# Neighbourhood attention with keys on partitions, and a runtime branch between two forms of it

## The chip, the core and the metric

The kernel runs on one core of a Trainium2 chip, everything in float32. A core has TensorE (PE in the profile; PEld is its loading of the stationary operand, "weights"), VectorE (DVE), ScalarE (ACT), GpSimd (POOL) and SyncE (SP), which here only issues DMAs. SBUF and PSUM have 128 partitions. The metric is device time in microseconds (us), lower is better.

## What is computed

The input `x` is (2, 56, 56, 256). Layer 0 normalises it in 32 groups, applies neighbourhood attention (8 heads of 32 channels, a 7x7 window that is shifted inwards at the border, a learned bias per relative position) and adds the result to `x`. Layer 1, which the change doesn't touch, is a chunked linear attention and a mixture of 8 experts. The part that matters, cut:

```python
x = fold_in(key(seed), 1) normal, (2, 56, 56, 256)       # setup_inputs
ks = split(key(seed), 5)
wq = normal(ks[1], (256, 256)) * 0.02                    # wk, wv, rpb: ks[2], ks[3], ks[4]; biases zero
...
q = (gn(x) @ wq.T + bq) / sqrt(32);  k = gn(x) @ wk.T + bk;  v = gn(x) @ wv.T + bv
scores = einsum('bnijd,bnijkd->bnijk', q, k_window) + bias_window
ctx = einsum('bnijk,bnijkd->bnijd', softmax(scores), v_window)
x = x + ctx
```

`fold_in`, `split` and `key` are those of `jax.random`.

## The kernel before

Three stages follow each other.

Projections (lines 166 to 276 of the file). The group statistics are taken, then for each batch and each block of 448 pixels the projections q, k (channels on partitions, L231) and v (pixels on partitions, L262) are multiplied. q is scaled by VectorE (L242), k is copied out by ScalarE (L251), v by VectorE (L269), and all three are written to DRAM (`q_d`, `k_d`, `v_d`).

Neighbourhood attention (L348 to L550). The image is cut into tiles of 8x14 queries: 7 strips of rows, 4 tiles in a strip, 2 batches, so 56 tiles; each has a frame of up to 14x20 = 280 keys. The bias is spread once through DRAM (`rpb_d`, L366 and L371) and added to a mask for each kind of tile on GpSimd (`bc`, L414). A unit is one tile and one group of 4 heads, 112 units. For each of its heads, `scores` multiplies queries by keys (L455: 32 rows of the array, 112 stationary columns, up to 280 moving ones), adds the bias and takes the row minimum of the negated scores in one VectorE instruction (L464), and takes the exponential with the row's sum on ScalarE (L474). `transposes` turns the exponentials with the array in two or three pieces for each head (L491) and copies them out of PSUM (L497, L499). `values` multiplies them with v (L510), and at the second group divides by the sums (L519, L521), adds `x` (L525) and writes `x1_d` with 8 DMAs from ScalarE's queue (L529). The last loop is a software pipeline over units: scores of unit n, transposes of n-1, values of n-2.

Layer 1 (from L551) reads `x1_d` (L618) and runs 14 steps; its chunk attention and the experts of earlier steps (L1170 to L1214) are interleaved by generators.

The loop that sets the order of the attention stage:

```python
for unit in chain(units(), (None, None)):
    if unit is not None:
        unit[0](unit[3])
    under_way.append(unit)
    if len(under_way) > 1 and under_way[-2] is not None:
        under_way[-2][1](under_way[-2][3])
    if len(under_way) > 2:
        done = under_way.pop(0)
        done[2](done[3])
```

Within an engine instructions run in the order in which the program lists them; across engines semaphores hold back whoever needs data or a buffer.

Of the kernel before, what the change touches and what calls it, by code (L numbers as in the profile page):

```python
# [32 lines left out]
QR, QC = 8, 14  # L33
TT = QR * QC
FR, FC = QR + WIN - 1, QC + WIN - 1
FK = FR * FC
NSR, NSC = IMG // QR, IMG // QC
# [35 lines left out]
def frame(start, size):  # L73

    lo, hi = max(start - WIN // 2, 0), min(start + size + WIN // 2, IMG)
    return lo, hi, lo - (start - WIN // 2)
# [6 lines left out]
def constants():  # L83
# [36 lines left out]
    mask = np.zeros((3, 3, TT, FK), np.float32)  # L120
    starts = (0, 1, -1)
    for er in range(3):
        r0 = QR * (starts[er] % NSR)
        rlo, rhi, _ = frame(r0, QR)
        for ec in range(3):
            c0 = QC * (starts[ec] % NSC)
            clo, chi, _ = frame(c0, QC)
            m = np.full((QR, QC, rhi - rlo, chi - clo), MASKED, np.float32)
            for a in range(QR):
                i = window_start(r0 + a) - rlo  # L130
                for b in range(QC):
                    j = window_start(c0 + b) - clo
                    m[a, b, i : i + WIN, j : j + WIN] = 0
            m = m.reshape(TT, -1)
            mask[er, ec, :, : m.shape[1]] = m
    c["nmask"] = mask
    return c


@with_exitstack  # L140
def hybrid_kernel(ctx: ExitStack, tc: tile.TileContext, t: dict, out: bass.AP):
# [5 lines left out]
    k_d = dram.tile([NB, C, L], F32, name="k_d")  # L147
    v_d = dram.tile([NB, IMG, IMG, C], F32, name="v_d")
    x1_d = dram.tile([NB, IMG, IMG, C], F32, name="x1_d")
    rpb_d = dram.tile([QC, NH, FR + QR - 1, FC], F32, name="rpb_d")  # L150
# [13 lines left out]

    with (
# [15 lines left out]
        bv = load(gp, "bv", [TT, C], t["L0_conv_bv"].unsqueeze(0).to_broadcast([TT, C]))  # L181

# [31 lines left out]
        for b in range(NB):  # L214
            for i in range(nst):
# [11 lines left out]
                for w, bias, dst, what in ((wq, bq, q_d, "q"), (wk, bk, k_d, "k")):  # L227
                    for g in range(NG):
# [9 lines left out]
                        o = ev.tile([P, BLK], F32, tag=f"ev{what}", name=f"ev{what}")  # L238
                        if what == "q":


                            nc.vector.tensor_scalar(  # L242
                                o.rearrange("p (q r c) -> p r q c", q=NSC, r=QR),
                                ps.rearrange("p (r q c) -> p r q c", q=NSC, r=QR),
                                bias[:, g : g + 1],
                                -1.0 / math.sqrt(HD),
                                ALU.add,
                                ALU.mult,
                            )
                        else:  # L250
                            nc.scalar.activation(  # L251
                                o, ps, AF.Identity, bias=bias[:, g : g + 1]
                            )
                        nc.sync.dma_start(
                            out=dst[b, g * P : (g + 1) * P, cols], in_=o
                        )
                o = ev.tile([TT, BLK // TT, C], F32, tag="evv", name="evv")
                for j in range(BLK // TT):
# [10 lines left out]
                    nc.vector.tensor_add(o[:, j, :], ps, bv)  # L269
# [4 lines left out]
                    in_=o,  # L274
                )

# [71 lines left out]
    with (  # L348
        tc.tile_pool(name="na1", bufs=1) as p1,
        tc.tile_pool(name="na", bufs=2) as p2,  # L350
        tc.tile_pool(name="na3", bufs=3) as p3,
        tc.tile_pool(name="na_sc", bufs=3, space=PSUM) as ps_s,
        tc.tile_pool(name="na_pt", bufs=3, space=PSUM) as ps_t,
        tc.tile_pool(name="na_po", bufs=2, space=PSUM) as ps_o,
    ):


        NR = 2 * WIN - 1
        pr, pc = QR - 1 - WIN // 2, QC - 1 - WIN // 2
        rp = p1.tile([NH, NR, NR], F32, name="rp")  # L360
        nc.sync.dma_start(out=rp, in_=t["L0_conv_rpb"])
        pad = p1.tile([NH, FR + QR - 1, FC + QC - 1], F32, name="pad")
        nc.gpsimd.memset(pad, 0.0)
        nc.vector.tensor_scalar_mul(pad[:, pr : pr + NR, pc : pc + NR], rp, -1.0)
        for b in range(QC):
            nc.sync.dma_start(  # L366
                out=rpb_d[b], in_=pad[:, :, QC - 1 - b : QC - 1 - b + FC]
            )
        bias = p1.tile([TT, NH, FR, FC], F32, name="bias")
        for a in range(QR):  # L370
            nc.sync.dma_start(  # L371
                out=bias[a * QC : (a + 1) * QC],
                in_=rpb_d[:, :, QR - 1 - a : QR - 1 - a + FR, :],
            )

        def units():

            for s in range(NSR):
                r0 = s * QR
                rlo, rhi, fr = frame(r0, QR)  # L380
                nr = rhi - rlo
                kw = p2.tile([P, NB, NG, FR * IMG], F32, tag="kw", name="kw")
                qw = p2.tile([P, NB, NG, QR * IMG], F32, tag="qw", name="qw")
                for b in range(NB):
                    nc.sync.dma_start(
                        out=kw[:, b, :, : nr * IMG],
                        in_=k_d[b, :, rlo * IMG : rhi * IMG].rearrange(
                            "(g p) l -> p g l", p=P
                        ),
                    )  # L390
                    nc.sync.dma_start(
                        out=qw[:, b],
                        in_=q_d[b, :, r0 * IMG : (r0 + QR) * IMG].rearrange(
                            "(g p) l -> p g l", p=P
                        ),
                    )
                last = bc = None
                for c in range(NSC):
                    clo, chi, fc = frame(c * QC, QC)
                    ncol = chi - clo  # L400
                    if edge(c, NSC) != last:
                        last = edge(c, NSC)
                        bc = tile_bias(edge(s, NSR), last, fr, nr, fc, ncol)
                    for b in range(NB):
                        yield from tile_units(
                            b, r0, c, rlo, nr, clo, ncol, kw[:, b], qw[:, b], bc
                        )

        def tile_bias(er, ec, fr, nr, fc, ncol):
            nk = nr * ncol  # L410
            msk = p2.tile([TT, FK], F32, tag="msk", name="msk")
            nc.sync.dma_start(out=msk, in_=t["nmask"][er, ec])
            bc = p2.tile([TT, NH, FK], F32, tag="bc", name="bc")
            nc.gpsimd.tensor_tensor(  # L414
                bc[:, :, :nk].rearrange("p h (r c) -> p h r c", c=ncol),
                bias[:, :, fr : fr + nr, fc : fc + ncol],
                msk[:, :nk]
                .rearrange("p (r c) -> p r c", c=ncol)
                .unsqueeze(1)
                .to_broadcast([TT, NH, nr, ncol]),  # L420
                ALU.add,
            )
            return bc

        def tile_units(b, r0, c, rlo, nr, clo, ncol, kw, qw, bc):
            c0, chi, nk = c * QC, clo + ncol, nr * ncol

            nj = -(-nr // (P // ncol))
            rows = [nr // nj + (j < nr % nj) for j in range(nj)]
            at = [sum(rows[:j]) for j in range(nj)]  # L430
            vw = p3.tile([P, 3, C], F32, tag="vw", name="vw")
            for j in range(nj):
                for r in range(rows[j]):
                    nc.sync.dma_start(
                        out=vw[r * ncol : (r + 1) * ncol, j, :],
                        in_=v_d[b, rlo + at[j] + r, clo:chi, :],
                    )
            xq = p3.tile([TT, C], F32, tag="xq", name="xq")
            for a in range(QR):
                nc.sync.dma_start(  # L440
                    out=xq[a * QC : (a + 1) * QC, :],
                    in_=t["x"][b, r0 + a, c0 : c0 + QC, :],
                )
            low = p3.tile([TT, NH], F32, tag="low", name="low")
            den = p3.tile([TT, NH], F32, tag="den", name="den")
            kept = {}

            def scores(g):
                sc = p2.tile([TT, 4, FK], F32, tag="sc", name="sc")
                ex = p3.tile([TT, 4, FK], F32, tag="ex", name="ex")  # L450
                for h in range(4):
                    hh = g * 4 + h
                    hp = slice(h * HD, (h + 1) * HD)
                    ps = ps_s.tile([TT, FK], F32, tag="ps", name="ps")
                    nc.tensor.matmul(  # L455
# [46 lines left out]
            def values(g):  # L502
# [14 lines left out]
                if g < NG - 1:  # L517
                    return
# [835 lines left out]
```

## Time and profile before

| | us |
|---|---|
| three runs | 3101.17, 3108.82 (median), 3118.96 |
| the profiled execution | 3124.91 |
| its span in the profile | 3122.9 |

| engine | busy in the span, us |
|---|---|
| PE (PEld) | 2450.1 (1729.7) |
| DVE | 1318.1 |
| ACT | 1033.5 |
| POOL | 646.4 |

The page's slices of the span show where the stages lie (each digit is one fortieth of the span, in tenths; PEclk is the clock granted to TensorE, 5 is half):

```
PE   6959978878797877767787887887887888885376
PEclk9955555555555555877888888888888898786688
DMA  5441111111112111000022222222222222123344
```

A float32 matrix product shows as two records of PE, a transpose as one. "Granted clock" is a share of the full clock. A table by stretches of the span gives, for each engine, busy microseconds and, in brackets, the number of instructions.

### The profile page before, as it was taken

Reading aid. Unit: us, or ns where it says so; the run is one execution under the profiler, and the core shown is the slowest. Engines: PE = TensorE matmul, PEld = TensorE weight load, DVE = VectorE, ACT = ScalarE, POOL = GpSimd, SP = SyncE. Lnnn points to the kernel's source line nnn. Section 1 sums busy time; section 2 is a strip of 40 time slices with the busy share of each in tenths; the row PEclk is TensorE's granted clock in tenths of the full one; section 3 lists DMA queues with packets and bytes.
Section 4 is the critical chain, followed back from the end, with each engine's and each line's share of the span. In section 5 each row is a group of like instructions: output and inputs, shape, how many; then the busy total and the mean of one; then the engine's idle time right before and its main releaser. Section 6 shows DMA issues by size and latency. Waiting matters only on the chain. (4 is left out here: it accounts for less than half of the span.)

```text
span 3122.9 us, 37893 instructions
## 1 busy us (share of the span) xinstructions
PE 2450.1 (78%) x13028; PEld 1729.7 (55%) x13028; DVE 1318.1 (42%) x4238; ACT 1033.5 (33%) x2268; POOL 646.4 (21%) x593
## 2 busy tenths in 40 slices
PE   6959978878797877767787887887887888885376
PEld 3647766767575766334454544555555555553254
DVE  5323323222222222566656556556655655651000
ACT  1123323232222222434344444444443544421011
POOL 0010011010101011121132232232233223222222
PEclk9955555555555555877888888888888898786688
DMA  5441111111112111000022222222222222123344
GB/s 206 150 112 30 30 59 30 52 37 40 46 28 61 27 58 37 1 25 17 9 81 64 49 80 64 53 78 64 62 68 66 63 65 82 42 68 105 95 111 104
DMA packets 136063, 196.50 MB, mean 63 GB/s; under 512 B 30368, under 2 KB 120432, under 8 KB 128192
## 3 DMA queue, kind: packets, MB, share of 16 engines
q1 hardware_dynamic: 100672, 153.58, 15.7%
q0 software_dynamic: 22368, 30.85, 5.8%
q10 hardware_dynamic: 12832, 9.66, 1.0%
q8 instruction: 104, 1.70, 0.2%
q14 instruction: 87, 0.71, 0.1%
HBM read 130.85 MB, written 63.14 MB: 62 GB/s over the span
## 5 line engine op out<-in xcount | busy, mean ns | idle before, releaser
L510 PEld LDWEIGHTS po<-vw,pT 100*112 100x112 f32 (+5 forms) x2112 | 410.5, 307 | 19.0 <-issue 11.4
L455 PE MATMUL ps<-kw,qw 32*112 32x238 f32 (+3 forms) x896 | 270.9, 674 | 190.4 <-DVE low L464 153.1
L510 PE MATMUL po<-vw,pT 100*112 100x32 f32 (+5 forms) x2112 | 409.3, 368 | 3.8 <-ACT pT L499 3.8
L474 ACT ACTIVATE ex<-sc,low 112x238 f32<-112x238 f32 (+3 forms) x448 | 218.5, 488 | 501.6 <-DVE low L464 276.6
L464 DVE CUSTOM_DVE_ANT_0 sc<-ps,bc 112x238 f32<-112x238 f32 (+3 forms) x448 | 167.2, 408 | 421.5 <-PE ps L455 265.9
L1214 POOL DMA_INDIRECT out<-ye,xg x112 | 176.6, 1577 | 616.6 <-DVE ye L1213 300.9
L1193 PE MATMUL p_h<-xT_g,wj 128*128 128x256 f32 x896 | 253.4, 430 | 60.7 <-DMA wj<-in_we 59.0
L455 PEld LDWEIGHTS ps<-kw,qw 32*112 32x112 f32 x896 | 119.4, 281 | 255.8 <-DVE low L464 170.3
L1193 PEld LDWEIGHTS p_h<-xT_g,wj 128*128 128x128 f32 x896 | 184.1, 215 | 115.5 <-issue 79.0
L491 PE MATMUL pt<-ident,ex 112*100 112x112 f32 (+5 forms) x1056 | 240.5, 406 | 0.0
L491 PEld LDWEIGHTS pt<-ident,ex 112*100 112x100 f32 (+5 forms) x1056 | 195.5, 241 | 79.8 <-ACT ex L474 44.4
L1205 PE MATMUL p_y<-wj,hT 128*128 128x256 f32 x896 | 226.0, 399 | 2.0 <-ACT hT L1200 2.0
L780 ACT ACTIVATE km<-p_kt,cmask 112x512 f32<-112x512 f32 x364 | 219.2, 725 | 6.3 <-PE p_kt L777 6.3
L525 POOL TENSOR_TENSOR xo<-ov,xq 112x256 f32<-112x256 f32 x56 | 40.5, 724 | 853.3 <-DVE ov L521 706.6
L1205 PEld LDWEIGHTS p_y<-wj,hT 128*128 128x128 f32 x896 | 172.4, 198 | 35.1 <-ACT hT L1200 7.5
L1200 ACT ACTIVATE hT<-p_h,wj 128x256 f32<-128x256 f32 x224 | 105.2, 482 | 249.1 <-PE p_h L1193 248.8
L906 DVE TENSOR_TENSOR own<-near,own 32x104 f32<-32x104 f32 x448 | 117.3, 262 | 132.2 <-PE near L895 125.8
L1179 DVE SCALAR_TENSOR_TENSOR own_e<-cand,l_exp,xg 128x8 f32<-128x8 f32 x112 | 25.8, 231 | 327.1 <-DMA xg<-xs_d 325.1
L1029 POOL DMA_INDIRECT xs_d<-xs,rowi x112 | 106.3, 949 | 274.4 <-DMA xs_d<-xs,rowi 126.7
L895 PEld LDWEIGHTS near<-qh,zs 128*32 128x32 f32 x2912 | 109.4, 118 | 90.6 <-DVE zs L884 39.8
L862 PE MATMUL p_z<-km,vt 112*32 112x448 f32 x896 | 147.4, 624 | 8.4 <-ACT km L780 7.6
L497 DVE COPY pT<-pt 119x448 f32<-119x448 f32 (+4 forms) x152 | 94.8, 624 | 124.5 <-PE pt L491 124.1
(230 smaller groups left out, 3650.7 us busy)
## 6 DMA issues: line engine op xcount, KB each, us to landing
wj<-in_we SPq DMA_DIRECT2D x56, 1026.0 KB
xg<-xs_d SPq DMA_DIRECT2D x56, 272.0 KB
kw<-k_d SPq DMA_DIRECT2D x10, 784.0 KB
vw<-v_d SPq DMA_DIRECT2D x368, 20.0 KB
xq<-in_x SPq DMA_DIRECT2D x448, 14.0 KB
x_d<-xo ACTq DMA_DIRECT2D x448, 14.0 KB
q_d<-evq SPq DMA_DIRECT2D x28, 224.0 KB
k_d<-evk SPq DMA_DIRECT2D x28, 224.0 KB
```

The source lines that it names most:

```text
L455: nc.tensor.matmul(ps[:, :nk].rearrange("p (r c) -> p r c", c=ncol), lhsT=qw[hp, g, c * TT : (c + 1) * TT], rhs=kw[hp, g, : nr * IMG].rear ...
L464: nc.vector.tensor_tensor_reduce(sc[:, h, :nk], ps[:, :nk], bc[:, hh, :nk], scale=1.0, scalar=-LOWEST, op0=ALU.add, op1=ALU.min, accum_out ...
L474: nc.scalar.activation(ex[:, h, :nk], sc[:, h, :nk], AF.Exp, bias=low[:, hh : hh + 1], scale=-1.0, accum_out=den[:, hh : hh + 1],)
L491: nc.tensor.transpose(pt[:n, h, :], ex[:, h, at[j] * ncol : at[j] * ncol + n], ident[:TT, :TT],)
L510: nc.tensor.matmul(po[:, hh, :], lhsT=pT[:n, j, h, :], rhs=vw[:n, j, hh * HD : (hh + 1) * HD], start=j == 0, stop=j == nj - 1,)
L780: nc.scalar.activation(km[:, :, :, c, :], pt.rearrange("p i (h e) -> p i h e", h=4), AF.Copy, scale=1.0 if c == NCH - 1 else cmask[:, c : ...
L862: nc.tensor.matmul(pz[hp], lhsT=vt[:, i, hp], rhs=km[:, i, h], start=True, stop=True,)
L895: nc.tensor.matmul(near[i * HD : (i + 1) * HD, :, c * CH : (c + 1) * CH], lhsT=zs[:, c - 1, :], rhs=qh[:, :, i * TT + c * CH : i * TT + (c ...
L906: nc.vector.tensor_tensor(own[hp, cols], near[i * HD : (i + 1) * HD, h, CH:], own[hp, cols], ALU.add,)
L1193: nc.tensor.matmul(ph, lhsT=w1[:, k, f * P : (f + 1) * P], rhs=xT[:, k, :], start=k == 0, stop=k == NG - 1,)
L1205: nc.tensor.matmul(py, lhsT=hT[:, f, u * P : (u + 1) * P], rhs=w2[:, f, :], start=f == 0, stop=f == NF - 1,)
L1214: nc.gpsimd.indirect_dma_start(out=out[:, :], out_offset=bass.IndirectOffsetOnAxis(ap=xg[:, u, TOK : TOK + 1].bitcast(U32), axis=0), in_=y ...
```

## The change

Layer 0 is rewritten; layer 1 stays.

- q is scaled by +1/sqrt(32) instead of the negative, in blocks of 8x8 queries. k isn't written to DRAM any more: ScalarE copies it into SBUF (`kc`) seven times in parts, once for each column of tiles, with a frame of 14 columns, 7 instructions of 128x112 in place of one of 128x448. v is laid out with 33 columns for each head, the 33rd being one, so that the product with v also gives the sum of the exponentials.
- Four maxima are kept: VectorE takes the largest absolute value of q and of k for every block (`tensor_reduce` of 128x448), of the bias table and of `bk`. At the end `32 * max|q| * max|k| + max|rpb|`, a bound on every score, is compared with `SAFE = 50`, all engines load the result into a register, and a branch is taken on it.
- The bias with its mask is spread on the host, in two layouts, and loaded.
- Tiles are 8x8 queries (49 of them), both batches together, each with a frame of 14x14 = 196 keys in two halves of 98.
- If the bound is below 50: for each group of 4 heads, 8 products put 98 keys on partitions and 2 heads x 64 queries in 128 columns (64 rows of the array), VectorE adds the bias (98x1024), ScalarE takes the exponential without a maximum (98x1024), and 16 products with v follow directly, without transposes.
- Else: for each head and each batch, 2 score products (queries stationary, 98 keys moving), the bias, a row maximum, the exponential, 2 transposes, 2 copies, 2 products with v.
- Both end in `finish`: reciprocal, product, `x` added on GpSimd, 2 DMAs to `x1_d`, now from SyncE's queue.

The core of the diff; lines that fall away are those of the stage described above.

```diff
+SAFE = 50.0
...
+                        for j in range(NT):
+                            f = frame(j)
                             nc.scalar.activation(
-                                o, ps, AF.Identity, bias=bias[:, g : g + 1]
+                                kv[:, j], pk[:, :, f : f + FT], AF.Identity, bias=bias[:, g : g + 1]
                             )
+                        nc.vector.tensor_reduce(
+                            top[:, 1, at : at + 1], ps, AX.X, ALU.max, apply_absolute_value=True
                         )
...
+        nc.vector.tensor_mul(mx[:, 0:1], mx[:, 0:1], mx[:, 1:2])
+        nc.vector.scalar_tensor_tensor(
+            mx[:, 0:1], mx[:, 0:1], float(HD), mx[:, 2:3], ALU.mult, ALU.add
+        )
+        safe = kp.tile([1, 1], I32, name="safe")
+        nc.vector.tensor_single_scalar(safe, mx[:, 0:1], SAFE, ALU.is_lt)
...
+    flag = nc.values_load(safe, min_val=0, max_val=1, ...)
+    with tc.If(flag > 0) as fast:
+            def scores(i, j, g, qb):
+                sc = ps_s.tile([P, 2, NB, 2, 2, QN], F32, tag="sc", name="sc")
                 for b in range(NB):
+                    for k in range(2):
+                        for p in range(2):
+                            rows = slice(p * 2 * HD, (p + 1) * 2 * HD)
+                            nc.tensor.matmul(
+                                sc[:KN, p, b, k],
+                                lhsT=keys(i, j, k, b, rows, g),
+                                rhs=qb[rows, g, :, b, :],
...
+                nc.scalar.activation(ex[:KN], ex[:KN], AF.Exp)
...
+            def context(ex, g, vw, po):
+                for p in range(2):
+                    for h in range(2):
+                        hh = g * 4 + p * 2 + h
+                        for k in range(2):
+                            for b in range(NB):
+                                nc.tensor.matmul(
+                                    po[b * QN : (b + 1) * QN, hh, :],
+                                    lhsT=ex[:KN, p, b, k, h, :],
+                                    rhs=vw[:KN, b, k, hh * (HD + 1) : (hh + 1) * (HD + 1)],
...
+    with fast.Else():
+            for i, j, qb, vw, xq in tile_rows(p2):
+                for hh in range(NH):
+                    bias = p2.tile([QN, FT * FT], F32, tag="bias", name="bias")
+                    nc.sync.dma_start(
+                        out=bias, in_=t["rpb_q"][kind, :, hh * FT * FT : (hh + 1) * FT * FT]
+                    )
                     for b in range(NB):
+                        ps = ps_s.tile([QN, FT * FT], F32, tag="ps", name="ps")
+                        for k in range(2):
+                            nc.tensor.matmul(
+                                ps[:, k * KN : (k + 1) * KN],
+                                lhsT=qb[hp, g, h % 2, b, :],
+                                rhs=keys(i, j, k, b, hp, g),
...
+                        nc.vector.tensor_tensor(sc, ps, bias, ALU.add)
+                        nc.vector.tensor_reduce(high, sc, AX.X, ALU.max, negate=True)
+                        nc.scalar.activation(sc, sc, AF.Exp, bias=high)
+                        for k in range(2):
+                            nc.tensor.transpose(
+                                pt[:KN], sc[:, k * KN : (k + 1) * KN], ident[:QN, :QN]
+                            )
+                            nc.vector.tensor_copy(pT[:KN], pt[:KN])
+                            nc.tensor.matmul(
+                                po[b * QN : (b + 1) * QN, hh, :],
+                                lhsT=pT[:KN],
+                                rhs=vw[:KN, b, k, hh * (HD + 1) : (hh + 1) * (HD + 1)],
...
+                finish(p2, i, j, po, xq)
```

In the Else part `ps`, `sc`, `bias`, `pt`, `po` and the loads `vw` and `xq` have two buffers each. In the built order SyncE's queue holds 8 bias loads (64x196), 4 of `vw`, 2 of `xq` and 2 writes of `x1_d` for each tile. TensorE's order for one head of both batches (first e, then o) settles into this, with the scores running two products ahead:

```
pt_e pt_e | ps | po_e | pt_o | po_e | pt_o | ps ps | po_o po_o | ps
```

## The prediction

> **What bounds the kernel now.** First the table of three stretches: projections, attention stage, layer 1.
>
> ```profile
> 199.00:1236.00 1037.00, 873.23 (x4058) 713.67 (x4058) 291.32 (x1160) 291.59 (x1009) 120.56 (x77) 0.50 0.14 41
> 0.00:165.00 165.00, 135.80 (x452) 84.07 (x452) 71.39 (x152) 19.25 (x30) 5.34 (x21) 1.00 0.51 177
> 165.00:199.00 34.00, 1.26 (x8) 0.48 (x6) 0.74 (x2) 0.00 (x0) 3.62 (x2) 0.54 0.67 158
> 1236.00:3122.00 1886.00, 1439.84 (x8512) 931.49 (x8512) 954.67 (x2924) 722.63 (x1229) 516.87 (x494) 0.82 0.24 63
> ```
>
> After the length come PE, PEld, DVE, ACT and POOL, then the granted clock, the DMA share and GB/s. The attention stage takes 1037 us of the 3123; TensorE is busy for 873 of them (84%), VectorE and ScalarE for 28% each. TensorE sets the stage, at clock 0.50 from its start to its end. The waits in it tell where the other 16% are:
>
> ```profile
> ACT ex L474 <- DMA x_d<-xo: 173.7, 21, 11.4
> ...
> PE ps L455 <- DVE low L464: 153.1, 67, 14.4
> ```
>
> TensorE waits 153 us for VectorE, because the score buffers are full; ScalarE's waits behind its own DMA issues lie mostly under TensorE's work. Then TensorE's timeline, at half clock (start, length of the run, records), for the price of a record:
>
> ```profile
> 367.04 0.61 PE L491 MATMUL pt<-ident,ex 112*100 112x112 f32 x2
> ...
> 369.93 4.18 PE L510 MATMUL po<-vw,pT 100*112 100x32 f32 x22
> ...
> 375.25 2.48 PE L491 MATMUL pt<-ident,ex 112*100 112x112 f32 x12
> 377.52 4.56 PE L510 MATMUL po<-vw,pT 100*112 100x32 f32 x24
> ```
>
> ```profile
> 1397.56 1.60 PE L895 MATMUL near<-qh,zs 128*32 128x32 f32 x26
> ```
>
> Ten more transposes take 2.48 - 0.61 = 1.87 us: 0.187 each, with 100 stationary and 112 moving columns. Two more value records take 4.56 - 4.18 = 0.38: 0.19 each, with 112 stationary and only 32 moving columns. L895, also at half clock, has 32 and 32: (1.60 - 0.22 for the last one) / 25 = 0.055. So a record costs 0.187 / 112 = 1.67 ns for each column of the wider operand; a narrow moving operand saves nothing. The same engine around a change of form:
>
> ```profile
> 207.83 3.06 PE L510 MATMUL po<-vw,pT 102*112 102x32 f32 x16
> 210.82 0.97 PE L455 MATMUL ps<-kw,qw 32*112 32x187 f32 x6
> 212.24 0.96 PE L455 MATMUL ps<-kw,qw 32*112 32x187 f32 x2 [0.45 <-DVE low L464]
> 213.13 1.18 PE L491 MATMUL pt<-ident,ex 112*102 112x112 f32 x5
> ```
>
> The last record of the first run starts at 210.51, so the next, on 32 rows instead of all, comes 0.31 later instead of 0.19: 0.12 lost. The pair at 212.24 starts its second record 0.44 to 0.45 later, where 187 columns at 1.67 ns are 0.31: 0.14 lost on the first weights. From that record (212.68) to the transposes are 0.45 instead of 0.31: 0.14. Going from one row size to another costs 0.14 to 0.26 us, say 0.2. Six records of three heads in 0.97 us show that different row groups run side by side; one head's don't.
>
> **Which branch.** The bound decides it, and the inputs decide the bound. `x` comes from `fold_in(key, 1)`, `wq` from `split(key, 5)[1]`. With the generator's present default the two keys are the same: evaluating `setup_inputs`, the 256 rows of `wq` are 0.02 times the first 256 pixels of `x`, to 2e-5. So a pixel meets its own copy among the rows: q there is about 0.02 x 256 / sqrt(32) = 0.9 where chance gives 0.29. Evaluated, max|q| = 1.183, max|k| = 1.730, max|rpb| = 0.079: 32 x 1.183 x 1.730 + 0.079 = 65.5, not below 50. The change takes Else, the per-head form with maximum and transposes. With keys split the older way the same evaluation gives max|q| = 0.287 and a bound of 16.0.
>
> **The change part by part**, on the path through Else.
>
> Projections: ScalarE copies k in 7 parts. A 128x448 copy lasts 0.63 (L251) and one of 187 columns 0.44 (L474), so 112 columns some 0.38: 14 x 0.38 = 5.3 us a block, against 9.7 for TensorE (135.80 / 14 blocks). VectorE gets four maxima at 0.61 (L834, 128x448 reduced): 2.4 more on 3 to 4. Both lie under TensorE's 9.7. A k buffer is held longer, 5.3 of 9.7 us, and there are four: 0 to 18 us (14 x 1.3), if the fourth product waits.
>
> Handover: the 34 us without TensorE (bias through DRAM) go. In their place: some ten small VectorE and TensorE operations (0.16 to 0.6 each, about 3 us), a register load and branch, then behind it what was prefetched before: 8 loads of q and 8 of v, `x` and bias at 0.4 of issue each (7 us) and a landing of 2.9 (L361, issued at 166.19, used at 169.04). That is 13 us and the branch. The nearest row for a register load is SyncE's at L1153, 0.38; no taken branch over thousands of instructions is in the trace. I bound the handover by -20 and +20 with the line above and take 0: the stage starts at 199 again. [...]
>
> Attention, one head of both batches (392 of them: 49 tiles x 8), on TensorE at half clock:
> - scores: 4 products of two records, 98 moving columns over 64 stationary ones: 8 x 98 x 1.67 ns = 1.31 us. All on one row group, so none side by side.
> - transposes: 4 records with 98 stationary columns: 0.65.
> - values: 4 products of two records, 64 columns: 8 x 0.107 = 0.85.
> - together 2.81. The three kinds use 32, 64 and 98 rows, and the built order has 9 groups for a head, so 9 changes of form: 9 x 0.2 = 1.8 (1.26 to 2.3).
>
> So 4.61 us, and 392 x 4.61 = 1807 us. VectorE has for a head two bias additions on 196 (0.36, between L464's 350 and 383 ns), two maxima on 196 (0.35; L1124 needs 325 ns for 176), four copies of 64 columns (0.22; L906 needs 262 ns for 104): 2.3 us. ScalarE: two exponentials at 0.45 (L474): 0.9. Both lie under 4.61. The dependent chain too: after the copies for o, the next head's maximum (0.35), exponential (0.45) and two handovers (0.1 each) take 1.0, while TensorE still has po_o and a score product, 1.2 us. The writes of `x1_d` move to SyncE, ahead of later bias loads; a head's bias is loaded two heads early (some 5 us against 2.9 of landing), so I take 0 for it. A head's fewer columns (64 x 196 x 2 against 112 x 238) buy nothing: the count of heads rises from 448 to 784.
>
> Sum: 199 + 1807 + 1886 = 3892 us of span, against 3122.9. Run and span differ by 2, and the profiled run lies 16 above the median: 3892 + 2 - 16 = 3878, rounded 3880.
>
> [...] The row shows 0.50 for 1037 us with TensorE 84% busy, in the same mix of narrow products and transposes that Else has; I go by the row. [...]
>
> **The rivals.**
>
> The fast branch is taken (other side): if the measured inputs come from independent keys, bound 16. Then 98 units: scores 16 records x 128 columns = 3.4 us, two row groups side by side: 1.7; values 32 records x 0.107 = 3.4, or 1.7 if the two halves of the columns overlap (L862 starts records on four column groups within 0.01 us); two changes of form 0.4. 3.8 to 5.5 us a unit, 373 to 540 in all, VectorE (1.2) and ScalarE (1.1) under it: 199 + 456 + 1886 = 2541, so about 2530. For it: nothing in the profile depends on the values. Against it: the evaluation. It decides as soon as the bound is under 50.
>
> The clock rises in Else: at 1.0 the records halve (1.4), the changes cost 0.15 (L862 to L876 and back), and the chain of waits through VectorE and ScalarE (0.36 + 0.35 + 0.45 + 0.4 for a transpose + four copies, and handovers) binds at about 2.7 us a head: 392 x 2.7 = 1058, so 3130 to 3160. Against it: the row at 0.50.
>
> SyncE's queue binds: if at each tile's end the next bias waits for the write ahead of it, that is reciprocal, product and addition (0.19 + 0.43 + 0.72) and a landing of 2.9: 4.2 x 49 = 208 us, 4090. It lies inside my range.
>
> **How the numbers follow.** Forecast with the third rival inside 0.81, fast branch 0.12, full clock 0.06, anything else 0.01. Range: with a change of form at 0.1 us the stage is 392 x 3.71 = 1454 (3525), and half of its way down to none at all (1102, 3175) gives 3350; with 0.26 it is 2020 (4090), and half of the queue's 208 on top gives 4200. Slower holds the forecast and nearly all of the full clock, which at 3130 to 3160 may just be the same. One measurement can't tell less than 0.5% from no change. Faster 0.12, same 0.03, slower 0.85.
>
> **What would show it.** In the new profile: exponentials of 64x196 (784 of them) and none of 98x1024; a stage of some 1800 us at clock 0.50 with TensorE the engine that is waited for; transposes about 0.16 apart and changes of form about 0.2. The forecast is wrong if 98x1024 appears, if the clock is 1.0, or if TensorE waits for bias or VectorE on most heads; layer 1 should still take 1886.

## The result and the profile after

| | before | after |
|---|---|---|
| median of the runs, us | 3108.82 | 3661.39 (3661.15 to 3662.72) |
| ratio to before, 95% interval | 1 | 1.1775 (1.1721 to 1.183) |
| span of the profiled execution | 3122.9 | 3659.4 |

The changed kernel is 18% slower. First the table of stretches, cut where the stages meet. After the length come PE, PEld, DVE, ACT and POOL (busy us, instructions), the granted clock, the DMA share and GB/s:

```profile
0.00:166.00 166.00, 136.56 (x457) 84.44 (x458) 102.87 (x214) 50.92 (x198) 8.02 (x24) 1.00 0.39 132
166.00:185.00 19.00, 1.88 (x12) 1.31 (x9) 1.05 (x5) 0.00 (x0) 6.10 (x2) 0.65 0.40 112
185.00:1774.00 1589.00, 1581.27 (x7832) 1094.84 (x7832) 778.69 (x3234) 359.63 (x785) 36.09 (x50) 0.50 0.14 37
1774.00:3659.00 1885.00, 1438.41 (x8512) 932.52 (x8512) 952.54 (x2924) 721.99 (x1229) 515.17 (x494) 0.82 0.24 63
```

The projections end at 166 (165 before), the handover takes 19 us (34), layer 1 takes 1885 (1886). All of the loss is the attention stage: 1589 us where it was 1037. In it TensorE is busy for 1581 us, 99.5%, at clock 0.50 from end to end. Which branch ran is told by the groups of instructions by line (shape, count, busy us and mean ns):

```profile
L567 PE MATMUL ps<-kc,qb 32*64 32x98 f32 x3136 | 807.5, 385 | 18.9 <-POOL qb L417 9.8
L578 ACT ACTIVATE sc<-sc,high 64x196 f32<-64x196 f32 x784 | 358.3, 457 | 1224.8 <-DVE high L577 1155.1
L585 DVE COPY pT<-pt 98x64 f32<-98x64 f32 x1568 | 312.2, 220 | 750.3 <-PE pt L581 750.3
L586 PE MATMUL po<-vw,pT 98*64 98x33 f32 x3136 | 578.3, 302 | 1.3 <-DVE pT L585 1.3
```

784 exponentials of 64x196 are 392 heads for each of two batches: Else. The last column, idle time ahead of the instruction, says who sets the pace: ScalarE and VectorE idle for hundreds of us, TensorE for a few. TensorE's timeline for one head of both batches (start, length of the run, records) shows what its time goes on:

```profile
600.71 0.91 PE L567 MATMUL ps<-kc,qb 32*64 32x98 f32 x4
601.54 0.64 PE L586 MATMUL po<-vw,pT 98*64 98x33 f32 x4
602.11 0.58 PE L567 MATMUL ps<-kc,qb 32*64 32x98 f32 x2
602.62 0.45 PE L581 MATMUL pt<-ident,sc 64*98 64x64 f32 x2
603.00 0.58 PE L567 MATMUL ps<-kc,qb 32*64 32x98 f32 x2
603.51 0.42 PE L586 MATMUL po<-vw,pT 98*64 98x33 f32 x2
603.86 0.34 PE L581 MATMUL pt<-ident,sc 64*98 64x64 f32 x1
604.13 0.42 PE L586 MATMUL po<-vw,pT 98*64 98x33 f32 x2
604.48 0.34 PE L581 MATMUL pt<-ident,sc 64*98 64x64 f32 x1
604.75 0.42 PE L567 MATMUL ps<-kc,qb 32*64 32x98 f32 x1
```

From scores to scores are 604.75 - 600.71 = 4.04 us, with nine changes between scores, transposes and values, as the prediction had them; 392 x 4.04 = 1584. Runs of different length give the price of one record: four score records last 0.91 and two 0.58, so a record is 0.165; four value records 0.64 and two 0.42, so 0.11.

### The profile page after: what moved, and what is told of

It is laid out like the page before. It is cut to its first block, busy times and chain, and to the rows that moved or that the text cites. A ratio compares the mean times of both kernels' runs of the same rounds, so it can differ in the third digit from the quotient of the medians.

```text
span 3659.4 us, 48361 instructions
## 1 busy us (share of the span) xinstructions
PE 3158.1 (86%) x16810; PEld 2113.1 (58%) x16810; DVE 1835.1 (50%) x6376; ACT 1132.5 (31%) x2212; POOL 565.4 (15%) x569
## 5 line engine op out<-in xcount | busy, mean ns | idle before, releaser
L567 PE MATMUL ps<-kc,qb 32*64 32x98 f32 x3136 | 807.5, 385 | 18.9 <-POOL qb L417 9.8
L578 ACT ACTIVATE sc<-sc,high 64x196 f32<-64x196 f32 x784 | 358.3, 457 | 1224.8 <-DVE high L577 1155.1
L585 DVE COPY pT<-pt 98x64 f32<-98x64 f32 x1568 | 312.2, 220 | 750.3 <-PE pt L581 750.3
L586 PE MATMUL po<-vw,pT 98*64 98x33 f32 x3136 | 578.3, 302 | 1.3 <-DVE pT L585 1.3
L586 PEld LDWEIGHTS po<-vw,pT 98*64 98x64 f32 x3136 | 420.9, 209 | 225.3 <-DVE pT L585 98.0
L567 PEld LDWEIGHTS ps<-kc,qb 32*64 32x64 f32 x3136 | 460.1, 205 | 142.2 <-POOL qb L417 10.1
L581 PE MATMUL pt<-ident,sc 64*98 64x64 f32 x1568 | 438.2, 331 | 2.3 <-ACT sc L578 2.3
L581 PEld LDWEIGHTS pt<-ident,sc 64*98 64x98 f32 x1568 | 215.1, 166 | 142.0 <-ACT sc L578 81.7
L575 DVE TENSOR_TENSOR sc<-ps,bias 64x196 f32<-64x196 f32 x784 | 269.3, 344 | 19.0 <-DMA bias<-in_rpb_q 18.3
L577 DVE TENSOR_REDUCE high<-sc 64x1 f32<-64x196 f32 x784 | 268.8, 343 | 12.9
```

Of the source, the lines that this page charges most:

```text
L567: nc.tensor.matmul(ps[:, k * KN : (k + 1) * KN], lhsT=qb[hp, g, h % 2, b, :], rhs=keys(i, j, k, b, hp, g), start=True, stop=True,)
L575: nc.vector.tensor_tensor(sc, ps, bias, ALU.add)
L577: nc.vector.tensor_reduce(high, sc, AX.X, ALU.max, negate=True)
L578: nc.scalar.activation(sc, sc, AF.Exp, bias=high)
L581: nc.tensor.transpose(pt[:KN], sc[:, k * KN : (k + 1) * KN], ident[:QN, :QN])
L585: nc.vector.tensor_copy(pT[:KN], pt[:KN])
```

## The experiments

All have the medians of their own runs; ratios are to runs of before on the same chip.

**e1 and e2, the branch.** One line each: `SAFE = 50.0` becomes 66.0 and 65.0.

> SAFE is 66 in place of 50; nothing else differs. If the inputs decide (bound 65.5), the first branch runs: 98 exponentials of 98x1024 and no transposes in the attention stage, 3.8 to 5.5 us for each of 98 units at half clock, so 2430 to 2610 us in all; below 2430 if the clock rises there. Rival, another cause for Else than the bound of 65.5 (the flag read wrongly, the maxima taken too large): 3661 again.

> SAFE is 65. If the bound is 65.5, Else runs as with 50: 3661 us. Together with 66 this brackets the bound between 65 and 66. Rival, a bound between 50 and 65: the first branch and some 2500 us.

Measured: e1 2458.08 (ratio 0.7919, 0.7892 to 0.7946), e2 3660.3 in a single run. So the bound lies between 65 and 66, as evaluated, and the threshold alone decides between 2458 and 3660. e1's stretches, and its TensorE timeline:

```profile
187.00:570.00 383.00, 358.88 (x4656) 325.71 (x4656) 148.71 (x196) 104.75 (x99) 34.78 (x49) 0.55 0.37 109
570.00:2455.00 1885.00, 1432.74 (x8512) 926.90 (x8512) 952.03 (x2924) 721.90 (x1229) 516.76 (x495) 0.82 0.24 63
```

```profile
196.58 1.92 PE L521 MATMUL po<-vw,ex 98*64 98x33 f32 x32
198.43 2.03 PE L497 MATMUL sc<-qb,kc 64*98 64x128 f32 x16
200.39 1.92 PE L521 MATMUL po<-vw,ex 98*64 98x33 f32 x32
```

Two batches of four heads take 200.39 - 196.58 = 3.81 us. Thirty-two value records take 1.85 from their start to the next run's: 0.058 each, where one after another they would take 0.107. They run two at a time.

**e3, fewer changes of form.** In Else both batches' scores, transposes and values are listed together:

```diff
-                            pt = ps_t.tile([P, QN], F32, tag="pt", name="pt")
+                    pt = ps_t.tile([P, NB, 2, QN], F32, tag="pt", name="pt")
...
-                            nc.vector.tensor_copy(pT[:KN], pt[:KN])
+                    nc.vector.tensor_copy(pT[:KN], pt[:KN])
+                    for b in range(NB):
+                        for k in range(2):
                             nc.tensor.matmul(
                                 po[b * QN : (b + 1) * QN, hh, :],
```

> Else with the products of both batches of a head put together: 4 score products into one PSUM tile, 4 transposes into one tile with one copy for all, then 4 products with v. TensorE's records stay the same (2.81 us a head), its changes of form fall from 9 to 4. Theory, changes of form are what a head costs beyond its records: 4 of them 0.05 to 0.18 each, 0.58 together, 3.4 us a head, 392 x 0.65 less, about 3400 us. Rival, waits for VectorE and ScalarE or the bias loads fill the time instead: 4.05 us a head stays or grows, 3650 or more.

Measured: 3211.97 (ratio 1.0346, 1.0328 to 1.0363), some 190 us less than I expected. One head on TensorE:

```profile
603.27 0.65 PE L590 MATMUL po<-vw,pT 98*64 98x33 f32 x8
603.85 0.66 PE L583 MATMUL pt<-ident,sc 64*98 64x64 f32 x4
604.44 1.56 PE L567 MATMUL ps<-kc,qb 32*64 32x98 f32 x8
605.93 0.33 PE L590 MATMUL po<-vw,pT 98*64 98x33 f32 x2
```

Eight value records last 0.65 here, as long as four did in after: batch 0 writes the first 64 rows of `po`, batch 1 the other 64, which I read as the two halves of the array's columns, and next to each other they run in pairs. The head takes 605.93 - 603.27 = 2.66 us with three changes. The transposes show a second thing: four last 0.66, two 0.45 in after, 0.105 each. That is 64 columns at 1.67 ns; I had priced them by their 98 stationary columns, 0.163.

**e4, the rows.** `qb` is zero outside a head's 32 rows of every second block, so Else's scores can use 64 rows as the fast branch does:

```diff
-                    hp = slice(h * HD, (h + 1) * HD)
+                    rows = slice(h // 2 * 2 * HD, (h // 2 + 1) * 2 * HD)
...
-                                lhsT=qb[hp, g, h % 2, b, :],
-                                rhs=keys(i, j, k, b, hp, g),
+                                lhsT=qb[rows, g, h % 2, b, :],
+                                rhs=keys(i, j, k, b, rows, g),
```

> Else with the score products on 64 rows of the array in place of 32 (the other head's 32 rows of the stationary operand are zeros, so the sums are the same). Scores and transposes then use the same number of rows, but 64 and 98 columns. If a change of the row size is what costs, the three passages between scores and transposes become free, 0.34 us a head, 133 in all: 3528. If the column size counts as well: 3661. If zeros on more rows cost time by themselves: over 3661.

Measured: 3664.75 (ratio 1.1798, 1.1779 to 1.1818), no difference. Scores on 64 rows and transposes on 64 rows still pay for the change (the step from a score record to a transpose is 0.295 us in after and 0.297 here), so it isn't the number of rows alone that makes one.

**e5, the pairs taken away.** e3, with each batch's values in a PSUM tile of its own, so that both use the same 64 columns (the division by the sums then runs once for each batch):

```diff
-                po = ps_o.tile([P, NH, HD + 1], F32, tag="po", name="po")
+                po = [ps_o.tile([QN, NH, HD + 1], F32, tag=f"po{b}", name="po") for b in range(NB)]
...
-                                po[b * QN : (b + 1) * QN, hh, :],
+                                po[b][:, hh, :],
```

> The Else form of e3 (products of a kind grouped, both batches' values next to each other), with the values of both batches now on the same 64 columns of the array, in two PSUM tiles; the order on TensorE and the number of changes of form stay as in e3. e3 came to 3212 where fewer changes of form alone gave some 3400. Theory (the rest came from values on different column halves running side by side: in e3's trace they start in pairs 14 ns apart, four products in 0.36 us where after needs 0.85): the pairs fall apart, 0.49 us a head, 392 x 0.49 = 192 us more, about 3400. Rival (the rest came from cheaper changes of form or fewer waits, and the column halves don't matter): 3212 as in e3, within 30.

Measured: 3402.94 (ratio 1.0893, 1.0852 to 1.0934). The theory said 3400, the rival 3212. The timeline:

```profile
602.05 0.66 PE L603 MATMUL pt<-ident,sc 64*98 64x64 f32 x4
602.63 1.56 PE L587 MATMUL ps<-kc,qb 32*64 32x98 f32 x8
604.13 1.06 PE L610 MATMUL po<-vw,pT 98*64 98x33 f32 x8
605.12 0.66 PE L603 MATMUL pt<-ident,sc 64*98 64x64 f32 x4
```

Values 1.06 instead of 0.65, a head 3.07 instead of 2.66, TensorE's order otherwise equal. So e3's gain has two parts: 3403 - 3212 = 191 us from pairs, and 3661 - 3403 = 258 us from fewer changes. The stage of e5 and then of e3:

```profile
185.00:1515.00 1330.00, 1248.38 (x7824) 1028.34 (x7824) 648.75 (x2155) 341.78 (x785) 38.10 (x51) 0.50 0.17 44
185.00:1322.00 1137.00, 1080.52 (x7788) 863.69 (x7786) 603.52 (x2045) 341.54 (x782) 34.70 (x48) 0.50 0.19 52
```

Between them TensorE's busy time falls by 168 us, 0.43 a head, where the theory had 0.49; that the sum still came to 191 is in part luck, since e3 also idles less (56 us against 82). In the steady order a change costs 0.16: e5's head of 3.07 less scores 8 x 0.163, transposes 4 x 0.107 and values 8 x 0.107 leaves 0.48 for three changes; after's 4.04 less the same leaves 1.45 for nine. The whole stage agrees: counted over all 392 heads after makes 8.9 changes a head and e5 3.5, and TensorE's busy time falls from 1581 to 1248 us, 333 / (392 x 5.4) = 0.16. Only 258 us of it reach the kernel's time, because TensorE idles 82 us in e5's stage and 8 in after's. e5 changes the PSUM tile along with the columns; products on two halves in two tiles weren't tried.

**e6, scores in pairs as well.** Both batches in one score tile of 128 rows, so that addition, maximum and exponential are done once for both (the bias of all heads is now loaded once a tile):

```diff
-                        ps = ps_s.tile([QN, FT * FT], F32, tag="ps", name="ps")
+                    ps = ps_s.tile([P, FT * FT], F32, tag="ps", name="ps")
...
+                            nc.tensor.matmul(
+                                ps[b * QN : (b + 1) * QN, k * KN : (k + 1) * KN],
...
+                    for k in range(2):
+                        nc.tensor.transpose(pt[:KN, k], sc[:, k * KN : (k + 1) * KN], ident)
```

> Else with both batches on the partitions of one score tile: batch 0's scores on the first 64 columns of the array, batch 1's on the other 64, alternating; bias addition, maximum and exponential once for both (128x196), two transposes of 128 rows for a head, one copy, values in pairs. Theory (products on different column halves run side by side, a record costs 1.67 ns a column at half clock, a change of form 0.14): scores 0.66, transposes 2 x 0.21, values 0.36, four changes 0.5: 1.95 us a head, 392 x 1.95 = 764; 185 + 764 + 1884 = 2830. Rival 1 (scores of one row group don't run side by side, whatever their columns): 2.6 us a head, 1020, 3090. Rival 2 (with TensorE this short the chain through VectorE and ScalarE sets the head: addition, maximum, exponential, transposes, copy and handovers, some 2.9 us with two heads under way): also some 1.5 to 2.0 a head, so 2700 to 2850, but then with TensorE waiting for VectorE or ScalarE on most heads.

Measured: 2921.65 (ratio 0.9352, 0.9316 to 0.9388), 90 us over the theory. It keeps the maximum and the transposes, so it needs no bound, and it beats before. Two heads:

```profile
599.72 0.66 PE L580 MATMUL pt<-ident,sc 128*98 128x128 f32 x2
600.31 0.91 PE L566 MATMUL ps<-kc,qb 32*64 32x98 f32 x6
601.16 0.67 PE L580 MATMUL pt<-ident,sc 128*98 128x128 f32 x2
601.75 0.65 PE L585 MATMUL po<-vw,pT 98*64 98x33 f32 x8
602.33 0.92 PE L566 MATMUL ps<-kc,qb 32*64 32x98 f32 x8
603.17 0.64 PE L585 MATMUL po<-vw,pT 98*64 98x33 f32 x8
603.75 0.58 PE L566 MATMUL ps<-kc,qb 32*64 32x98 f32 x2
604.26 0.45 PE L580 MATMUL pt<-ident,sc 128*98 128x128 f32 x1
```

Eight score records last 0.92 where e5's last 1.56: they pair up too, so rival 1 is out. Two heads take 604.26 - 599.72 = 4.54, with seven changes. For one of them transposes come between the first score product and its partner (the runs of 2 and 6 records), so that these two run alone, at 2 x 0.163 each: records are 0.65 + 0.98 for scores, 0.86 for transposes and 0.86 for values, 3.35. The changes share the other 1.19, 0.17 each, as in after and e5. Over the whole stage a head takes 853 / 392 = 2.18 us instead of 1.95. The theory lacked three things, some 100 us together: values at 0.43 for 0.36 (27 us), 108 score products that stand apart from their partners (0.33 each, 35 us), and 38 us in which TensorE idles. Its 0.5 for changes holds, since three a head at 0.17 (counted over the stage) come to what it had for four. Rival 2 is out as well: TensorE is busy 815 us of the stage's 853.

**e7, e9, e10, the clock.** After with a dense filler of equal TensorE time for each head, its result unused: two products on the whole array with 512 moving columns (e7), the same on 32 rows by 32 columns (e9), or eight of 128 columns on the whole array (e10).

```diff
+                    dn = ps_d.tile([P, 512], F32, tag="dn", name="dn")
+                    for _ in range(2):
+                        nc.tensor.matmul(dn, lhsT=ident, rhs=kc[:, 0, 0, 0, :512], start=True, stop=True)
```

> after, with two more products for each head in Else, 128 rows by 128 columns by 512 moving columns, whose result isn't used; they are only there to keep the whole array at work. TensorE is busy 99.7% of the attention stage in after and the clock stays at 0.50 throughout. At half clock the two cost 4 records x 512 x 1.67 ns = 3.4 us a head and two to four more changes of form, 0.3 to 0.5. Theory (the clock goes by how much of the array works, not by how long TensorE is busy): the clock in the stage rises well over 0.50, and the time is below 4700; at full clock throughout a head would take 3.9 us as before and the time 3620. Rival (in a stage of such short products the clock stays down whatever is added): 4.04 + 3.7 to 3.9 us a head, 392 x 3.8 = 1490 more, 5100 to 5200.

> e7 with its two added products for each head cut to 32 rows and 32 columns of the array; their 512 moving columns, and so the time for which they keep TensorE busy, are those of e7 (4 records x 512 x 1.67 ns = 3.4 us a head at half clock). e7 came to 4456 with the clock of the attention stage at 0.64 to 0.74, where after has 0.50 at the same busy time. Theory (the clock goes by how much of the array works): 0.50 throughout, 4.04 + 3.4 + 0.3 us a head, 392 x 3.7 = 1450 more than after, 5100. Rival (long moving operands release the clock, however little of the array they use): 4350 to 4550 as e7, with the clock near 0.7.

> e7 with its two added products of 512 moving columns for each head replaced by eight of 128 moving columns, on all 128 rows and 128 columns as there: the same work for the array in records as short as a 128-column score. Theory (share of the array at work): the clock rises as in e7, 0.6 to 0.75 in the stage, 4300 to 4700. Rival (length of the records): 0.50 throughout, some 5100.

Measured: e7 4456.43 (ratio 1.427, 1.4191 to 1.4348), e9 5071.0 (1.626, 1.6171 to 1.635), e10 4752.84 (1.524, 1.5154 to 1.5326). The same stretch of the three, in this order, the granted clock third from the end:

```profile
600.00:1400.00 800.00, 800.00 (x3126) 392.16 (x3126) 279.02 (x1072) 119.20 (x261) 11.55 (x16) 0.72 0.10 25
```

```profile
600.00:1400.00 800.00, 800.00 (x2485) 325.73 (x2484) 226.28 (x852) 95.27 (x207) 9.38 (x13) 0.50 0.07 19
```

```profile
600.00:1400.00 800.00, 800.00 (x4219) 635.78 (x4219) 242.25 (x967) 97.95 (x234) 10.16 (x14) 0.66 0.08 22
```

TensorE is busy 100% in all three. The clock rises where the filler fills the array, with long or short operands alike, and stays at 0.50 where it uses a sixteenth of it. The 0.72 is a mean: the clock switches between full and half. Two stretches of e7:

```profile
715.00:750.00 35.00, 35.00 (x178) 17.94 (x177) 15.93 (x62) 7.33 (x16) 0.72 (x1) 1.00 0.13 31
756.00:774.00 18.00, 18.00 (x59) 8.94 (x57) 5.15 (x20) 1.83 (x4) 0.00 (x0) 0.50 0.03 7
```

So in this stage the clock goes by how much of the array works, not by busy time. An estimate puts the runs in order: add up rows x columns x moving columns over a stage's records, at 1.67 ns a column, and divide by the whole array (128 x 128) over the stage's length. That gives 0.09 in e9, 0.12 in after and 0.29 in before, all at 0.50; 0.50 in e1, which has no transposes, at 0.55; 0.57 in e10 at 0.65 and 0.63 in e7 at 0.71, the clocks too being means over the stage. (A higher clock raises the share by itself, so these figures aren't a threshold, and e9 cut rows and columns together.) The filler doesn't pay for itself in any of them. e10 lies 50 over the range I had given it; why its clock is lower than e7's wasn't tried.

**e8, the guard.** e1's path alone, without the register load, the branch and Else, so without a way out where the bound is larger:

```diff
-    flag = nc.values_load(safe, min_val=0, max_val=1, ...)
-    with tc.If(flag > 0) as fast:
```

> e1's path (no maximum, no transposes) without the register load, the branch and the Else part; the four maxima and the comparison with SAFE are still computed, but nothing reads them. Theory (the branch stands between the projections and the attention stage and keeps loads and memsets from being issued early: in e1's trace the safe flag is there at 167.4, the first scores run at 176.5 and regular work starts at 187.7): the stage starts 10 to 15 us earlier, 2445. Rival (the loads of q and v wait for the projections' writes anyway, and the buffers for q for the projections' memory): 2458 as e1, within 5.

Measured: 2452.54 (ratio 0.7858, 0.7828 to 0.7888). The first bias addition of the stage, in e1 and then in e8 (start first):

```profile
186.38 2.36 DVE L506 TENSOR_TENSOR ex<-sc,bias 98x1024 f32<-98x1024 f32 x2 [18.96 <-DMA vw<-v_d]
```

```profile
184.47 1.22 DVE L502 TENSOR_TENSOR ex<-sc,bias 98x1024 f32<-98x1024 f32 x1 [16.87 <-PE sc L493]
```

Only 2 us sooner, and the first values as well (188.2 for 190.2). Clearing `qb` starts at 169.9 in e1 and 170.1 in e8, after the projections' last write in both; the first load is issued at 173.0 and 169.9, so without the branch the loads do go out 3 us sooner, in another order. The medians differ by 6 us with overlapping runs (2446 to 2457 and 2452 to 2469), and part of that is clock (0.60 in e8's stage, 0.55 in e1's). The two ran on different chips, and their ratios to before lie 0.006 apart, some 19 us, so the times set no close bound on what the branch costs; the trace shows 2 us at the start of the stage, nearer to the rival's "same" than to the theory's 10 to 15.

## Why the prediction was right

- *The branch.* Right: reading the keys of the random generator and evaluating the bound at 65.5 decided the sign. e1 and e2 bracket it. Without this step the diff reads as a change that takes the maximum and the transposes away, and the time would have been forecast at the fast branch's.
- *TensorE sets the stage, at half clock.* Right: busy 99.5% at 0.50. 1589 us at 99.5% busy didn't raise the clock, and e9 and e7 show what was missing, the share of the array: the filler on a corner left the clock at 0.50, the one on the whole array brought it to a mean of 0.72. Going by before's row rather than by the second rival (3130 to 3160) was worth some 500 us.
- *Scores 1.31 and values 0.85 a head.* Right: steady records of 0.163 and 0.107.
- *Transposes 0.65.* Wrong in size: 0.43. The rule "a record costs the wider operand" came from products, for which it held again (values: 64 stationary, 33 moving columns, 0.107), and from transposes whose moving side was the wider. In the new transposes the stationary side is, 98 to 64, and e3 shows 0.105 a record: they go by the moving side. 0.22 x 392 = 86 us.
- *Nine changes at 0.2.* The count is right, the size isn't: 0.16. Single passages in before's rows had shown 0.12 to 0.14; 0.2 was the middle of a range whose upper end is the sum of two of them. 0.35 x 392 = 137 us. Both together are 0.57 a head, and 4.61 - 0.57 = 4.04.
- *Stage start at 199.* 185: the handover took 19 us instead of 34, inside the bounds of 20 I had given. (The 0.38 of L1153, taken as the nearest row for a register load, is the issue of a DMA; the register operations of that line take 0.04.) Projections' extra work is hidden as said: ScalarE 51 and VectorE 103 of 166 us.
- *The 16 us taken off for the median.* Wrong: the profiled execution lay at after's median. In sum -14 (start), -218 (stage), -1 (layer 1), +14 (the 16 of the median, less 2 of rounding): 3880 becomes 3661. Every error but the last made the forecast too high.
- *VectorE, ScalarE, the chain and SyncE's queue under TensorE.* Right. The waits in the stage (from 220 to 1700 us), by who waits for whom:

```profile
ACT sc L578 <- DVE high L577: 1081.1, 420, 3.6
DVE pT L585 <- PE pt L581: 699.0, 1011, 1.1
...
DVE sc L575 <- DMA bias<-in_rpb_q: 0.8, 3, 0.4
```

After the line waited for come microseconds, times and the longest. The other engines wait for TensorE; for bias loads VectorE waits 0.8 us in all, so the third rival's 208 didn't occur.
- *The rivals.* The fast branch was priced at 2530 with 3.8 to 5.5 us a unit; e1 gives 3.81 and 2458, since the halves of the columns do overlap, which I had left open. For the full clock, 2.7 us a head, no clean run exists; e7 reached that clock for some stretches only (1.00 from 715 to 750 us).

## What to carry to other kernels

A guarded fast path is worth what the guard lets through: evaluate the bound on the real inputs before counting its gain, and choose the threshold by what overflows (a sum of 196 exponentials of 66 is some 1e31, far below float32's limit) rather than by caution; here 50 against 66 is 3661 against 2458. On TensorE with small products, list those of one kind together and alternate between halves of the columns: that took the safe path from 3661 to 2922, in e6 with addition, maximum and exponential of both batches in one instruction as well. Price records by start-to-start steps within a run and count the changes between kinds apart, each from rows with the same operand shapes.

## What the runs showed of the hardware

- A change between kinds of products costs 0.16 to 0.17 us at half clock in after, e5 and e6: the time of a head beyond the prices of its records, shared out over its changes, with no wait shown (in after the 384 steps from a value to a score record all take 0.225 to 0.227 us, where one value record to the next takes 0.106 to 0.130 in all but 7 of 1972 cases). No run here shows what happens in a change, and e4 leaves open which property of the form makes it (3664.75 against 3661.39 with scores on 64 rows in place of 32).
- Products of one group of rows on different halves of the columns run two at a time when they are adjacent: 8 value records in 0.65 instead of 1.06 us (e3, e5), 8 score records in 0.92 instead of 1.56 (e6, e5).
- The granted clock stays at 0.50 through 1589 us of 99.5% busy TensorE and rises to a mean of 0.72 by a filler on the whole array (e7), not by one of equal length on a corner of it (0.50 in e9).
- A register load and a branch ahead of the stage cost some 2 us at its start where the first body runs (e1 against e8). What the jump to Else costs wasn't measured apart: after's handover takes 19 us, as e8's without a branch.
